# State space recurrence on one core: the multiply by Cx on another engine, loads and sums in another order

## The chip, the cores and the metric

The kernel runs on one core of one Trainium2 chip, as a single launch. The core has five engines that work at the same time and meet through semaphores: TensorE (PE) for matmuls, VectorE (DVE) and ScalarE (ACT) for elementwise work, GpSimd (POOL) for elementwise work and some transfers, and SyncE (SP), which here only issues transfers. The metric is the device time of one execution in microseconds (us). Before the change it was 2233.52 us in the median of three runs, 2227.85 to 2237.58.

## The reference

Two batches of 1024 tokens with 128 features pass through eight residual blocks: latent attention, a spiking feed-forward, a state space block, the spiking feed-forward again, linear attention, experts, a softmax attention and the experts again. The change lies in the state space block:

```
A = -jnp.exp(A_log)
def step(h, inp):
    dt, b_t, c_t, x_t = inp
    A_bar = jnp.exp(dt[:, :, None] * A)
    h = A_bar * h + (dt * x_t)[:, :, None] * b_t[:, None, :]
    y = jnp.einsum('ben,bn->be', h, c_t)
    return (h, y)
_, y = jax.lax.scan(step, h0, xs)
y = y.transpose(1, 0, 2)
y = y + x * W_D
y = y * jax.nn.silu(skip)
y = jnp.einsum('ble,de->bld', y, out_w)
return resid + y
```

For each batch there are 256 channels (e) with 16 states (n) each, so 4096 independent recurrences over 1024 tokens.

## The kernel before

The recurrences of a batch are laid out as 32 tiles of 128 rows (8 channels times 16 states) by 1024 tokens. A tile is numbered t here; in its triple (e, s, r), e is the half of the channels, and r and s pick 8 of the half's 128 (rows 32r + 8s onward). Four tiles in a row (r = 0 to 3) form a group.

`StateSpace.loop` handles a tile like this:

- two transfers by SyncE (L759) bring the step sizes, broadcast over the 16 states, into `s_a` (4 buffers) and the inputs into `s_h` (8 buffers), each 512 KB;
- ScalarE makes the decays in place, exp(a * negA) (L768), one tile ahead of the scan;
- VectorE multiplies the inputs by Bx (L799), runs the recurrence as one scan along the tokens (L800) and multiplies the states by Cx (L801), all in place in `s_h`;
- TensorE sums the 16 states of each channel for a whole group with 16 small matmuls (L775, `s_py<-s_h,s_fold`). They are issued in the tile after the group's last. After them the group's four `s_h` buffers are free;
- after four groups `finish` (L785, L788) adds the direct path and multiplies by the gate, on VectorE.

The loads for tile t+3 are issued in tile t, in the order a, h.

The loop does not run alone. The whole first layer stands under a manual schedule: each engine executes its instructions in the order in which the program issues them. `weave` takes one step of the loop, then on average 2.1 steps of a second stream, and so on:

- Batch 0's loop (`space[0].loop`, L1500) has at its side the attention of batch 1 (`latent.attend`) and `late`, which makes the step sizes of the loop's second half (L713 to L724, with two stores by SyncE, L722 and L724, four times). `among` puts one `late` step after two attention steps until they are used up. A unit of attention is one head group c and one block of keys kb: matmuls L359 and L368, an exponential on ScalarE (L382, in two parts), for a diagonal block two selects on POOL (L385), and two units later the weighing and denominator matmuls on TensorE (L418, L401). The first half of the queries has 16 units, all diagonal; the second has 32, of which 16 are. At the end of a half come a reciprocal (L443), matmuls L450 and multiplies L454 or L458 on VectorE.
- Batch 1's loop (L1510) has at its side `late` and what is left behind batch 0: the end of its linear attention (L914 to L917, with an add on POOL, L917) and the first experts. An expert step is three matmuls of 128x512 (L963, L964, L979), a gate on ScalarE (L966) and a product on VectorE (L971), which reads one operand from PSUM.

What follows batch 1's loop, from about 1003 us on, is bound by TensorE: two more attentions and experts, in an order written out by hand.

Of the kernel before, what the change touches and what calls it, by code (L numbers as in the profile page):

```python
# [9 lines left out]
F32 = mybir.dt.float32  # L10
# [9 lines left out]
P = 128  # L20
B = 2
L = 1024
# [588 lines left out]
class StateSpace:  # L611


    EB, R, S, N, CH = 2, 4, 4, 16, 512
# [128 lines left out]
    def loop(self, work, bank):  # L743

        self.bank = bank
        g, w, nc, b, CH = self.g, self.w, self.g.nc, self.b, self.CH
        EB, R, S, N = self.EB, self.R, self.S, self.N
        chunks = [(n, bass.ts(n, CH)) for n in range(2)]

        yg = self.xc  # L750
        tiles = [(e, s, r) for e in range(EB) for s in range(S) for r in range(R)]

        def load(e, s, r):
            pages = []
            a = work.tile([P, L], F32, name="s_a", bufs=4)
            h = work.tile([P, L], F32, name="s_h", bufs=8)
            for k, t in enumerate((a, h)):
                rows = self.steps[e][k, 32 * r + 8 * s : 32 * r + 8 * s + 8, :]
                nc.sync.dma_start(  # L759
                    out=t, in_=rows.unsqueeze(0).to_broadcast([N, 8, L])  # L760
                )
                pages.append(t)
            return pages

        def decay(t, a):
            e, s, r = tiles[t]
            k = (e * R + r) * S + s
            nc.scalar.activation(a, a, AF.Exp, scale=self.shared.negA[:, k : k + 1])  # L768

        def sums(e, s, hcs):  # L770
            if s == 0:
                self.py = [self.bank("s_py") for _ in range(2)]
            for n, cols in chunks:
                for r in range(R):
                    nc.tensor.matmul(  # L775
                        self.py[n][32 * r : 32 * r + 32, :],
                        self.shared.fold[:, s, :],
                        hcs[r][:, cols],
                        start=(s == 0),
                        stop=(s == S - 1),  # L780
                    )

        def finish(e):
            for n, cols in chunks:
                nc.vector.scalar_tensor_tensor(  # L785
                    yg[:, e, cols], self.xc[:, e, cols], w["W_D"][:, e, :], self.py[n], ALU.mult, ALU.add
                )
            nc.vector.tensor_mul(yg[:, e, :], yg[:, e, :], self.gate[:, e, :])  # L788

        ahead = [load(*tiles[t]) for t in range(3)]  # L790
        decay(0, ahead[0][0])
        done, hcs = None, []
        for t, (e, s, r) in enumerate(tiles):
            if t + 3 < len(tiles):
                ahead.append(load(*tiles[t + 3]))
            a, h = ahead.pop(0)
            if t + 1 < len(tiles):
                decay(t + 1, ahead[0][0])
            nc.vector.tensor_mul(h, h, self.Bx)  # L799
            nc.vector.tensor_tensor_scan(h, a, h, 0.0, ALU.mult, ALU.add)  # L800
            nc.vector.tensor_mul(h, h, self.Cx)  # L801
            hcs.append(h)
            if done is not None:
                sums(*done)
                if done[1] == S - 1:
                    finish(done[0])
                done = None
            if r == R - 1:
                done, hcs = (e, s, hcs), []
            yield  # L810
        sums(*done)
        finish(EB - 1)
        yield
        for n, cols in chunks:
            po = self.bank("s_po").rearrange("p (a b) -> p a b", a=4)
            for t in range(4):
                for e in range(EB):
                    nc.tensor.matmul(
                        po[:, t, :],
                        yg[:, e, bass.ts(4 * n + t, P)],  # L820
                        w["out_wT"][:, e, :],
                        start=(e == 0),
                        stop=(e == EB - 1),
                    )
            xn = g.x[:, b * TPB + 4 * n : b * TPB + 4 * n + 4, :]
            nc.vector.tensor_add(xn, xn, po)
            yield
# [802 lines left out]
```

## Time and profile before

The profiled execution has a span of 2232.4 us, 1.1 us under the median of the runs. TensorE's mean granted clock in it was 0.940.

| engine | busy us | share | instructions |
|---|---|---|---|
| PE | 1966.3 | 88% | 13504 |
| DVE | 1656.4 | 74% | 1955 |
| ACT | 1303.7 | 58% | 1698 |
| POOL | 873.1 | 39% | 432 |

| operation | count | us each | sum us |
|---|---|---|---|
| L799 DVE multiply by Bx | 64 | 1.22 (median) | |
| L800 DVE scan | 64 | 2.323 (mean) | 148.7 |
| L801 DVE multiply by Cx | 64 | 1.225 (median) | |
| L768 ACT decays | 64 | 1.149 (median) | |
| L385 POOL selects in batch 0's loop | 64 | 1.366 (mean) | 85.8 |
| L854 POOL add, 128x1024 | 2 | 2.348 (mean) | 4.7 |
| L678 POOL add, 128x512 | 4 | 1.264 (median) | 5.1 |
| loads of s_a, to landing | 64 | 5.2 (median) | |
| loads of s_h, to landing | 64 | 6.5 (median) | |

How to read it: a busy share is a mean over stages with different limits, so a stage's own stretch must be looked at. In a timeline line the first number is the start in us from the beginning of the span, the second the duration, then engine, source line, operation, output and inputs by tile name, shapes, and a count; what stands in brackets is the idle time of the engine before it and what ended it. In a line of waits the three numbers are us in total, number of waits and the longest. A stretch's line gives the busy us (and instructions) of PE, PE's weight loads, DVE, ACT and POOL, then the granted TensorE clock, the busy share of the DMA engines and GB/s.

### The profile page before, as it was taken

How to read it: one execution, taken by the hardware profiler on the slowest of the kernel's cores; microseconds unless marked ns; L12 is line 12 of the kernel's file. 1: busy time of each engine (PE TensorE's matmuls, PEld its weight loads, DVE VectorE, ACT ScalarE, POOL GpSimd, SP SyncE). 2: the span in 40 equal slices, each digit the busy share in tenths (PEclk: the TensorE clock that was granted, in tenths of full speed). 3: DMA queues.
4: the chain of work that ended last, by engine and by line, in shares of the span. 5: the costliest groups of instructions: out<-in, count | busy, mean ns of one | idle time of the engine just before them, and what ended most of it. 6: DMA issues, size and time to landing. Idle time of an engine off the chain costs nothing. (4 is left out here: it accounts for less than half of the span.)

```text
span 2232.4 us, 33571 instructions
## 1 busy us (share of the span) xinstructions
PE 1966.3 (88%) x13504; PEld 1131.1 (51%) x13504; DVE 1656.4 (74%) x1955; ACT 1303.7 (58%) x1698; POOL 873.1 (39%) x432
## 2 busy tenths in 40 slices
PE   7779888979967758897788999999999999999999
PEld 4323243323334323344555667676676667766754
DVE  5866867898774699885325889888898889988322
ACT  1026612266633666754445888778888788877322
POOL 0013400064311000000100777777888778777500
PEclk9779978989998979998899999999999999999999
DMA  4000000197623287530002555665666656565200
GB/s 90 1 1 1 1 1 0 35 224 166 158 70 104 60 201 172 134 74 0 1 0 66 152 151 152 153 164 147 156 159 157 161 153 158 152 156 151 48 5 5
DMA packets 73787, 219.98 MB, mean 99 GB/s; under 512 B 9184, under 2 KB 19872, under 8 KB 73504
## 3 DMA queue, kind: packets, MB, share of 16 engines
q1 hardware_dynamic: 54736, 149.40, 22.8%
q0 software_dynamic: 18432, 67.12, 15.9%
q8 instruction: 106, 1.74, 0.3%
q10 hardware_dynamic: 464, 1.33, 0.3%
q14 instruction: 49, 0.40, 0.1%
HBM read 78.35 MB, written 5.24 MB: 37 GB/s over the span
## 5 line engine op out<-in xcount | busy, mean ns | idle before, releaser
L1277 POOL TENSOR_TENSOR h_e<-h_e,h_r 128x2048 f32<-128x2048 f32 x128 | 601.8, 4705 | 66.9 <-issue 60.4
L1248 DVE TENSOR_REDUCE h_m<-h_s 128x128 f32<-128x2048 f32 x128 | 292.8, 2288 | 88.8 <-PE h_s L1237 88.8
L1254 DVE TENSOR_TENSOR h_e<-h_s,h_m 128x2048 f32<-128x2048 f32 x128 | 293.2, 2291 | 9.6 <-DVE h_m L1248 0.4
L1269 PE MATMUL h_pd<-h_e,ident 128*128 128x256 f32 x1024 | 250.9, 388 | 25.8 <-DMA h_e<-h_e 25.4
L1257 ACT ACTIVATE h_e<-h_e 128x1024 f32<-128x1024 f32 x256 | 256.5, 1049 | 28.0 <-DVE h_e L1254 27.2
L1067 ACT ACT_TABLE_LOAD x134 | 171.9, 1283 | 104.6 <-PE e_pgu L1060 103.5
L1269 PEld LDWEIGHTS h_pd<-h_e,ident 128*128 128x128 f32 x1024 | 191.3, 192 | 63.6 <-issue 39.6
L385 POOL TENSOR_SCALAR_AFFINE_SELECT a_pT<-a_pT 128x256 f32<-128x256 f32 x120 | 130.3, 1108 | 206.7 <-ACT a_pT L382 203.8
L287 DVE TENSOR_REDUCE a_nm<-a_s 128x2 f32<-128x1024 f32 (+7 forms) x144 | 168.2, 1218 | 45.6 <-PE a_s L278 27.3
L1060 PE MATMUL e_pgu<-e_uT,Wg 128*128 128x256 f32 x640 | 196.4, 389 | 5.4 <-DVE e_h L1075 2.4
L1075 DVE TENSOR_TENSOR e_h<-e_sg,e_pgu 128x256 f32<-128x256 f32 x320 | 119.8, 404 | 106.7 <-ACT e_sg L1067 103.8
L1265 POOL DMA_DIRECT2D h_e<-h_e x128 | 114.4, 894 | 201.5 <-DMA h_e<-h_e 69.6
L1060 PE MATMUL e_pgu<-e_uT,Wu 128*128 128x256 f32 x640 | 192.5, 383 | 0.0
L1085 PE MATMUL h_po<-e_h,Wd 128*128 128x256 f32 x640 | 186.7, 408 | 3.5 <-DVE e_h L1075 2.3
L1067 ACT ACTIVATE e_sg<-e_pgu 128x256 f32<-128x256 f32 x320 | 112.3, 382 | 105.9 <-PE e_pgu L1060 90.4
L382 ACT ACTIVATE a_pT<-a_st 128x1024 f32<-128x1024 f32 (+3 forms) x176 | 129.9, 791 | 67.6 <-PE a_st L368 66.1
L1257 ACT ACT_TABLE_LOAD x128 | 164.2, 1283 | 2.3
L1085 PEld LDWEIGHTS h_po<-e_h,Wd 128*128 128x128 f32 x640 | 111.7, 193 | 102.3 <-issue 76.3
L800 DVE TENSOR_TENSOR_SCAN s_h<-s_a,s_h 128x1024 f32<-128x1024 f32 x64 | 148.7, 2323 | 18.0 <-ACT s_a L768 14.1
L269 PE MATMUL a_s<-a_latT,a_qT 32*128 32x512 f32 (+3 forms) x768 | 123.2, 621 | 39.3 <-DVE a_nm L287 37.4
L1237 PE MATMUL h_s<-h_qz,h_kT 32*128 32x512 f32 x1024 | 147.6, 646 | 9.8 <-DVE h_e L1254 7.9
L1282 PE MATMUL h_po<-h_e,h_vz 128*32 128x128 f32 x4096 | 138.4, 276 | 3.6 <-DVE x_res L1375 3.4
(290 smaller groups left out, 3066.2 us busy)
## 6 DMA issues: line engine op xcount, KB each, us to landing
h_e<-h_e SPq DMA_DIRECT2D x128, 512.0 KB, 4.7
h_e<-h_e POOLq DMA_DIRECT2D x128, 512.0 KB, 4.6
s_a<-s_steps SPq DMA_DIRECT2D x64, 512.0 KB, 5.2
s_h<-s_steps SPq DMA_DIRECT2D x64, 512.0 KB, 6.5
s_steps<-s_gate SPq DMA_DIRECT2D x8, 256.0 KB, 2.0
Wg<-in_Wg_dram SPq DMA_DIRECT2D x8, 256.0 KB, 6.0
Wu<-in_Wu_dram SPq DMA_DIRECT2D x8, 256.0 KB, 5.9
Wd<-in_Wd_dram SPq DMA_DIRECT2D x8, 256.0 KB, 6.1
```

The source lines that it names most:

```text
L287: nc.vector.tensor_reduce(nm[:, half, i, h : h + together], s[:, :, :n], AX.X, ALU.max, negate=True)
L800: nc.vector.tensor_tensor_scan(h, a, h, 0.0, ALU.mult, ALU.add)
L1060: nc.tensor.matmul(pgu[:, k, :], w[name][:, e, f], uT, start=True, stop=True)
L1067: nc.scalar.activation(sg, pgu[:, 0, :], AF.Silu)
L1085: nc.tensor.matmul(self.sums, self.w["Wd"][:, e, fc, :], h, start=False, stop=last, skip_group_check=True)
L1237: nc.tensor.matmul(s[:, j, :].rearrange("p (k q) -> p k q", k=K), kTs[b][quad, bass.ts(kb, P)], qzs[b][qb // 4][quad, :, bass.ts(qb % 4, P ...
L1248: nc.vector.tensor_reduce(m, heads.rearrange("p h q -> p q h"), AX.X, ALU.max)
L1254: nc.vector.tensor_sub(e, heads, m.unsqueeze(1).to_broadcast([P, H, P]))
L1257: nc.scalar.activation(eh, eh, AF.Exp, scale=scale)
L1269: nc.tensor.matmul(pd, g.ident, pair[:, :, k, :], start=(k == 0), stop=(k == 7))
L1277: nc.gpsimd.tensor_mul(e, e, r.unsqueeze(1).to_broadcast([P, H, P]))
L1282: nc.tensor.matmul(po[32 * j : 32 * j + 32, :], vz[:, kb * J + j, k].rearrange("p a d -> p (a d)"), a[:, 4 * j + k, :], start=False, stop= ...
```

## The change

Three things in `StateSpace.loop`:

- the multiply of the states by Cx is issued to POOL instead of VectorE;
- `load` brings one of the two pages; in tile t first the inputs of tile t+2, then the step sizes of tile t+3 are issued;
- a group's sums are issued in the second tile after its last one (r == 1 of the next group) instead of the first; with them `finish` of the first half of the channels. The last group's sums still stand directly after the loop.

```
-        def load(e, s, r):
-            pages = []
-            a = work.tile([P, L], F32, name="s_a", bufs=4)
-            h = work.tile([P, L], F32, name="s_h", bufs=8)
-            for k, t in enumerate((a, h)):
-                rows = self.steps[e][k, 32 * r + 8 * s : 32 * r + 8 * s + 8, :]
-                nc.sync.dma_start(
-                    out=t, in_=rows.unsqueeze(0).to_broadcast([N, 8, L])
-                )
-                pages.append(t)
-            return pages
+        def load(k, e, s, r):
+            t = work.tile([P, L], F32, name="s_h", bufs=8) if k else work.tile([P, L], F32, name="s_a", bufs=4)
+            rows = self.steps[e][k, 32 * r + 8 * s : 32 * r + 8 * s + 8, :]
+            nc.sync.dma_start(out=t, in_=rows.unsqueeze(0).to_broadcast([N, 8, L]))
+            return t
...
-        ahead = [load(*tiles[t]) for t in range(3)]
-        decay(0, ahead[0][0])
+        decays, inputs = [], []
+        for t in range(3):
+            decays.append(load(0, *tiles[t]))
+            if t < 2:
+                inputs.append(load(1, *tiles[t]))
+        decay(0, decays[0])
         done, hcs = None, []
         for t, (e, s, r) in enumerate(tiles):
+            if t + 2 < len(tiles):
+                inputs.append(load(1, *tiles[t + 2]))
             if t + 3 < len(tiles):
-                ahead.append(load(*tiles[t + 3]))
-            a, h = ahead.pop(0)
+                decays.append(load(0, *tiles[t + 3]))
+            a, h = decays.pop(0), inputs.pop(0)
             if t + 1 < len(tiles):
-                decay(t + 1, ahead[0][0])
+                decay(t + 1, decays[0])
             nc.vector.tensor_mul(h, h, self.Bx)
             nc.vector.tensor_tensor_scan(h, a, h, 0.0, ALU.mult, ALU.add)
-            nc.vector.tensor_mul(h, h, self.Cx)
+            nc.gpsimd.tensor_mul(h, h, self.Cx)
             hcs.append(h)
-            if done is not None:
+            if r == 1 and done is not None:
                 sums(*done)
                 if done[1] == S - 1:
                     finish(done[0])
```

## The prediction

> **What bounds the kernel now.** I read the page first, then busy time by stage for the stretches in which the changed loop runs, then VectorE's and POOL's timelines there, then the waits. Batch 0's loop runs from 450 to 662 us (attention of batch 1 beside it), batch 1's from 778 to 1003 us (experts beside it).
>
> ```profile
> span 2232.4 us, 33571 instructions
> ```
> ```profile
> core 0: us, PE busy (x) PEld busy (x) DVE busy (x) ACT busy (x) POOL busy (x), PEclk, DMA share, GB/s
> 450.00:517.00 67.00, 57.32 (x512) 20.04 (x514) 64.59 (x46) 47.44 (x62) 46.81 (x32) 0.87 0.97 226
> 517.00:640.00 123.00, 115.31 (x1022) 42.98 (x1022) 92.45 (x63) 72.90 (x90) 40.87 (x33) 0.99 0.62 146
> 778.00:821.00 43.00, 17.82 (x46) 7.08 (x46) 40.69 (x42) 24.42 (x29) 4.36 (x2) 0.67 0.92 214
> 821.00:1003.00 182.00, 165.07 (x444) 66.02 (x445) 161.49 (x155) 128.76 (x137) 0.00 (x0) 0.96 0.56 132
> ```
> Four regimes: VectorE sets the pace in 450-517 and 778-821 (96% and 95% busy), TensorE in 517-640 (94%); in 821-1003 the two are nearly level. POOL is free in batch 1's loop, but has 64 selects (L385) in batch 0's, half of them in its first 67 us.
>
> A tile with nothing between it and the next, and one with two expert products between:
> ```profile
> 652.76 1.22 DVE L799 TENSOR_TENSOR s_h<-s_h,s_Bx 128x1024 f32<-128x1024 f32 x1
> 654.08 2.29 DVE L800 TENSOR_TENSOR_SCAN s_h<-s_a,s_h 128x1024 f32<-128x1024 f32 x1
> 656.41 1.23 DVE L801 TENSOR_TENSOR s_h<-s_h,s_Cx 128x1024 f32<-128x1024 f32 x1
> 657.55 1.22 DVE L799 TENSOR_TENSOR s_h<-s_h,s_Bx 128x1024 f32<-128x1024 f32 x1
> ```
> ```profile
> 963.35 2.29 DVE L800 TENSOR_TENSOR_SCAN s_h<-s_a,s_h 128x1024 f32<-128x1024 f32 x1
> 965.68 1.22 DVE L801 TENSOR_TENSOR s_h<-s_h,s_Cx 128x1024 f32<-128x1024 f32 x1
> 966.82 1.28 DVE L971 TENSOR_TENSOR e_h<-e_sg,e_pu 128x512 f32<-128x512 f32 x2
> 968.02 1.22 DVE L799 TENSOR_TENSOR s_h<-s_h,s_Bx 128x1024 f32<-128x1024 f32 x1
> ```
> The Cx multiply takes 1.15 us from start to next start; the whole bare tile 4.79.
>
> **Price of the multiply on POOL.** The trace has POOL tensor-tensor rows of the same shape, and two places where a smaller one meets the loop:
> ```profile
> L854 POOL TENSOR_TENSOR l_u<-l_u,b_out 128x1024 f32<-128x1024 f32 x2 | 4.7, 2348 | 297.0 <-ACT l_un L84 297.0
> ```
> ```profile
> 784.49 1.22 DVE L799 TENSOR_TENSOR s_h<-s_h,s_Bx 128x1024 f32<-128x1024 f32 x1
> 784.65 2.18 POOL L917 TENSOR_TENSOR x_res<-x_res,l_u 128x512 f32<-128x512 f32 x1 [25.09 <-DVE l_u L916]
> ...
> 785.81 3.17 DVE L800 TENSOR_TENSOR_SCAN s_h<-s_a,s_h 128x1024 f32<-128x1024 f32 x1
> ```
> ```profile
> 545.46 1.88 POOL L471 TENSOR_TENSOR x_res<-x_res,a_rs 128x512 f32<-128x512 f32 x1 [1.33 <-ACT a_rs L470]
> ...
> 546.31 2.11 DVE L801 TENSOR_TENSOR s_h<-s_h,s_Cx 128x1024 f32<-128x1024 f32 x1
> ```
> POOL's 512-element add takes 1.26 alone (L678) but 2.18 here: it waits out L799, and then the scan takes 3.17 instead of 2.29. The second place repeats it with 2.11 for 1.23. So the two engines take turns on operations with two SBUF inputs, and a POOL add of 1.26 costs VectorE 0.88, its length less 0.38. The multiply of 2.35 then costs 1.97. Products that read one side from PSUM do not collide: L1277 on POOL keeps 4.7 for twice the size while VectorE runs L1254 undisturbed at 2.29.
>
> The Trainium skill ("SBUF — State Buffer", the section Summary: rules for kernel authors) goes further: the second operation blocks until the first has finished entirely. The rows show 0.38 less. By the rule each bare tile would lose another 0.38, an estimated 5 us over the sum; I keep the rows.
>
> **Sum by tile type.** Bare tile: VectorE loses 1.15 and waits 1.97, **+0.8**. Two expert products (1.2) between: POOL starts at the end of the scan and holds the next L799 until 2.3 (0.08 to start, 2.35 less 0.14 overlap) after it, where L799 started 2.4 after it: **-0.1**. More than 2.3 of harmless work or waiting between: **-1.15**. With batch-0 late sizes between: L717 reads one SBUF input and hides, L718/L719 must wait for POOL, 2.3+1.4 against 3.3, +0.4; L721 goes ahead of POOL and L723 behind, 0.7+2.1+0.7 against 2.75, +0.75.
>
> *450-517.* Tiles 0 to 10: seven bare (5.6), two each of the late kinds (0.8+1.5): VectorE is 7.9 late. TensorE feels it, because POOL works in order: the selects of attention units issued after tile t now wait behind multiply t, which waits for scan t; the weighing matmuls L418 wait for the selects, and everything after them on TensorE. The last selects of this half ended at 515.4. Now: scan 10 ends at 510.1+7.1, the next L799 goes first (1.2), multiply 2.35, two selects with one scan between (0.4+2.3+0.4) give 523.9, **+8.5**. If the six selects queued before it each wait out one VectorE operation at the contended mean of 1.37 us, it is about +12. I take **+10**; bounds +2 (TensorE keeps its lead) and +20 (43 POOL operations against some 30 of VectorE, which alternate).
>
> *517-640.* TensorE-bound; one head group takes 25.6 us (L434 at 577.33 and 602.91). The shared turn would hold 3.8 tiles x (3.51+1.97) + 8 selects x 0.41 = 24.2 of these. Selects that ended at 575.4 come some 4 later by laying operations in turn, in the next group 2.5; with quieter groups counted at less, +2 for each of four groups: **+8**; bounds 0 and +16. L458, on TensorE's way at 632, stands behind one multiply fewer: **-1**. The tail to 663 mixes -1.15 and +0.8: 0.
>
> *778-821.* Types sum to -0.3: **0**.
>
> *821-1003.*
> ```profile
> PE e_pu L964 <- DVE e_h L971: 19.8, 13, 7.0
> ```
> This row caps the gain: nothing VectorE gives back can exceed TensorE's 19.8 of waiting for it. Ten ordinary tiles at -0.1, one with statistics -1.15, one with the finish -0.3 make -2.5. Ten tiles where VectorE itself waits for ScalarE or TensorE could give -10 but TensorE paces them; I credit 1.5. **-4**, bounds -20 and +2.
>
> *Fetches and sums.* SyncE's order stays a, h, a, h; a pair leaves when scan t-4 is done (a at 453.55, h at 454.11 after the scan ending 453.52). Only the h next to a store (L722/L724) falls behind it, with three tiles (15 us) against 6.5 us to land: 0. If that cover went, a late h would cost up to its 6.5 at each of the eight places. The sums one tile later free eight h buffers a tile later, still three tiles before use; they meet multiply t+3's POOL latency (2.35 against 1.23), so TensorE's 4.2 us of waiting there in 450-517 is replaced by the selects' wait, counted above. After 1003 TensorE's order and work are unchanged and the difference is carried through.
>
> Total 10+8-1-4 = **+13**: the profiled execution, 2232.4 of span, becomes 2245.4. The median of the runs, 2233.5, is 1.1 over that span, so **2246 us**.
>
> **Rivals.**
> 1. *TensorE's lead absorbs the turns* (2234, chance 0.36). For it: TensorE waits only 4.2 for this loop in 450-517, and VectorE idles 30 of 123 us in 517-640. Against: order on POOL. Half 0 +5, groups +0, loop 2 -4, tail -1: +0.
> 2. *Faster: POOL's turns fall under expert products and VectorE hands them over sooner* (2218, chance 0.10). Place: 821-1003. For it: 55 products of 0.68 there do not collide and POOL is empty. It needs nearly all of the 19.8: -18, with batch 0 at +2. It decides if TensorE's waits on L971 fall below 5 us. Against: between scans 2.3 replaces 2.4.
> 3. *Selects starve* (2266, chance 0.12). POOL gets one operation per VectorE operation: +20 and +16, with -1 and -3. For it: 1.37 mean against 0.41 uncontended. Against: VectorE stalls when ScalarE's decays are late, and lets POOL through.
>
> **Numbers.** Forecast chance 0.42. About 0.5% (11 us) is what a measurement here can tell from no change. Slower by more: 0.42+0.12 = 0.54; within: 0.36; faster: 0.10. The range reaches down into rival 1 by the measured spread (2228) and up nearly to rival 3's time (2264).
>
> **What would show it.** L801 on POOL near 2.4 alone and above 3.5 where it waits; L800 or L799 long by 2; selects above 1.4; batch 0's loop ending near 680, batch 1's loop 4 shorter. Wrong if L800 stays at 2.29 with POOL busy, or if L418 does not wait on POOL.

## The result, and the profile after

The changed kernel takes 2250.46 us in the median of 12 runs (2231.71 to 2259.72), the kernel before 2230.11 in the median of 12 runs beside them (2224.41 to 2245.99). The medians are 20 us apart; the ratio between the two kernels' runs is 1.0072, with a 95% interval of 1.0048 to 1.0095: slower, by 16 us in 2230 (11 to 21). The profiled execution of the changed kernel has a span of 2249.1 us, against 2232.4 before. The page of the profile after, its head (busy us, share of the span, instructions) and the groups of the scan, of the multiply that moved and of the selects (out<-in, count | busy us, mean ns of one | idle before and what ended it):

```profile
span 2249.1 us, 33636 instructions
...
PE 1960.4 (87%) x13504; PEld 1128.8 (50%) x13504; DVE 1636.0 (73%) x1891; ACT 1303.9 (58%) x1698; POOL 1024.6 (46%) x496
...
L801 POOL TENSOR_TENSOR s_h<-s_h,s_Cx 128x1024 f32<-128x1024 f32 x64 | 171.1, 2675 | 266.5 <-DVE s_h L800 245.2
...
L800 DVE TENSOR_TENSOR_SCAN s_h<-s_a,s_h 128x1024 f32<-128x1024 f32 x64 | 168.7, 2637 | 25.7 <-ACT s_a L762 21.9
...
L385 POOL TENSOR_SCALAR_AFFINE_SELECT a_pT<-a_pT 128x256 f32<-128x256 f32 x120 | 111.9, 954 | 74.8 <-ACT a_pT L382 72.1
```

VectorE gave up 64 multiplies, 79.6 us in sum, but its busy time fell by only 20.4 (1656.4 to 1636.0). By the groups of both profiles the scans grew by 20.0 (148.7 to 168.7), the multiplies by Bx by 25.5 (80.7 to 106.2) and the late sizes L718 to L723 by 11.7: 57 of the missing 59 us are VectorE instructions of the same work that took longer, which is what waiting for turns with POOL looks like. POOL took on 171.1 us for work that fills 64 x 2.35 = 150.

The loops are cut here at the same events in every kernel: the first multiply by Bx, the reciprocals L443 that end the two halves of the attention, the end of the second L826 (the loop's result added in; a changed kernel's line may be a few lower) and, for batch 1, from its first multiply by Bx to its first L826. "Half 0" and "half 1" are the stretches that the prediction called 450-517 and 517-640, "tail" is the rest of batch 0's loop, "loop 2" batch 1's. The cuts are made at the starts in the timelines, the second L826 at its end; "repeat" is a later run of the changed kernel (an experiment below).

| us | half 0 | half 1 | tail | loop 2 | sum of changes |
|---|---|---|---|---|---|
| before | 67.9 | 106.9 | 50.6 | 227.0 | |
| after | 84.7 | 110.5 | 46.5 | 223.7 | |
| change | +16.8 | +3.7 | -4.1 | -3.3 | +13.1 |
| repeat | 83.3 | 109.6 | 52.0 | 223.6 | |
| change | +15.4 | +2.7 | +1.4 | -3.4 | +16.1 |

The loss lies in half 0. (The rounding of the cuts is 0.1.) Outside the loops the profile after differs too: 8.0 less before the loop and 14.9 more in the last softmax attention, both in code that the change does not touch. The repeat has 4.0 less and 3.2 more there, and over all the profiles of this case the attention takes 868 to 889 us, so these look like differences between executions.

The stretches half 0, half 1, tail and loop 2 of the profile after (us; busy us and instructions of PE, PEld, DVE, ACT, POOL; granted clock, DMA share, GB/s), and then half 0 and half 1 of the one before:

```profile
441.93:526.58 84.65, 66.14 (x514) 23.21 (x516) 65.19 (x35) 48.08 (x63) 69.79 (x44) 0.74 0.82 192
526.58:637.08 110.50, 105.32 (x968) 37.04 (x964) 75.49 (x38) 68.93 (x86) 78.50 (x48) 0.97 0.56 131
637.08:683.60 46.52, 28.95 (x148) 16.21 (x148) 38.23 (x42) 13.56 (x17) 13.43 (x6) 0.89 0.35 89
785.90:1009.60 223.70, 181.81 (x505) 74.91 (x506) 189.54 (x164) 152.98 (x166) 81.03 (x34) 0.89 0.62 149
```
```profile
449.90:517.80 67.90, 58.12 (x516) 20.26 (x516) 64.72 (x48) 48.18 (x63) 46.81 (x32) 0.87 0.98 227
517.80:624.70 106.90, 104.40 (x968) 37.11 (x964) 81.25 (x54) 68.90 (x86) 40.87 (x33) 1.00 0.65 152
```

In half 0 VectorE's busy time is the same although 13 instructions are gone (48 to 35), and POOL's has gone from 46.8 to 69.8 us. No engine is busy for nine tenths of the stretch any more.

VectorE's timeline at the start of half 0 (start, us, engine, line, operation), then POOL's:

```profile
443.25 2.29 DVE L800 TENSOR_TENSOR_SCAN s_h<-s_a,s_h 128x1024 f32<-128x1024 f32 x1
445.46 1.20 DVE L799 TENSOR_TENSOR s_h<-s_h,s_Bx 128x1024 f32<-128x1024 f32 x1
446.76 4.25 DVE L800 TENSOR_TENSOR_SCAN s_h<-s_a,s_h 128x1024 f32<-128x1024 f32 x1
```
```profile
445.62 3.24 POOL L801 TENSOR_TENSOR s_h<-s_h,s_Cx 128x1024 f32<-128x1024 f32 x1 [65.46 <-DVE s_h L800]
448.81 6.63 POOL L385 TENSOR_SCALAR_AFFINE_SELECT a_pT<-a_pT 128x256 f32<-128x256 f32 x4
455.41 2.79 POOL L801 TENSOR_TENSOR s_h<-s_h,s_Cx 128x1024 f32<-128x1024 f32 x1
```

The multiply waits out the next L799 (3.24 instead of 2.35), then the next scan waits for the multiply (4.25 instead of 2.29), and the four selects behind it in POOL's queue wait in turn for VectorE's operations: 6.63 us for four, where one alone takes 0.41.

The waits of half 0 (us, number, longest), 441 to 527 us after:

```profile
PEld a_oT L418 <- POOL a_pT L385: 21.5, 13, 5.9
PE a_oT L418 <- POOL a_pT L385: 13.4, 5, 5.5
DVE a_rec L443 <- ACT a_rec L442: 11.2, 1, 11.2
DVE s_xc L719 <- ACT s_xc L716: 7.1, 2, 3.8
```

Before, TensorE waited 0.2 us for the selects in this half, and its weight loads 2.8. Now the weighing matmuls stop for up to 5.5 us at a time, VectorE is idle 11.2 us before the reciprocal that closes the half, and for 7.1 us in the late sizes. The two idle times of VectorE do not show a loss by themselves: the kernel further down in which POOL only writes has 8.2 and 7.1 us at the same places and its half 0 is as short as before.

### The profile page after: what moved, and what is told of

The parts are those of the page before. It is cut to its first block, busy times and chain, and to the rows that moved or that the text cites. A ratio compares the mean times of both kernels' runs of the same rounds, so it can differ in the third digit from the quotient of the medians.

```text
span 2249.1 us, 33636 instructions
## 1 busy us (share of the span) xinstructions
PE 1960.4 (87%) x13504; PEld 1128.8 (50%) x13504; DVE 1636.0 (73%) x1891; ACT 1303.9 (58%) x1698; POOL 1024.6 (46%) x496
## 5 line engine op out<-in xcount | busy, mean ns | idle before, releaser
L801 POOL TENSOR_TENSOR s_h<-s_h,s_Cx 128x1024 f32<-128x1024 f32 x64 | 171.1, 2675 | 266.5 <-DVE s_h L800 245.2
L800 DVE TENSOR_TENSOR_SCAN s_h<-s_a,s_h 128x1024 f32<-128x1024 f32 x64 | 168.7, 2637 | 25.7 <-ACT s_a L762 21.9
L269 PE MATMUL a_s<-a_latT,a_qT 32*128 32x512 f32 (+3 forms) x768 | 116.1, 579 | 43.3 <-DVE a_nm L287 41.4
L385 POOL TENSOR_SCALAR_AFFINE_SELECT a_pT<-a_pT 128x256 f32<-128x256 f32 x120 | 111.9, 954 | 74.8 <-ACT a_pT L382 72.1
```

Source lines behind the costliest of these rows:

```text
L801: nc.gpsimd.tensor_mul(h, h, self.Cx)
```

## The experiments

Each ratio is to the kernel before, run beside it, with its 95% interval. In all but the first and the last but one, the fetches and the sums stand as in the change. Cx stands for the multiply L801.

### Which part costs

**Cx alone** (loads and sums as before):
```
-            nc.vector.tensor_mul(h, h, self.Cx)
+            nc.gpsimd.tensor_mul(h, h, self.Cx)
```


> The multiply by Cx goes to POOL and nothing else changes; loads and sums stay as before the change. Theory (turns on SBUF inputs, and the selects' place behind the multiplies on POOL): batch 0's loop from its first Bx multiply to the first reciprocal (67.9 us before the change, 84.7 with it) stays at 82 to 92, since TensorE now also stands at the sums until POOL's multiply of 2.35 us is done; the time is 1.005 to 1.012 of before. Rival (the later fetch or the later sums cost it): that stretch falls back to under 73 and the time to within 0.3% of before.

Ratio 1.0091 (1.0059 to 1.0123), half 0 83.3, half 1 113.5. **Loads and sums alone**, with Cx on VectorE:
```
-            nc.gpsimd.tensor_mul(h, h, self.Cx)
+            nc.vector.tensor_mul(h, h, self.Cx)
```


> Loads and sums as in the change, the multiply by Cx on VectorE as before it. Theory: neither costs or gains more than 2 us: the stretch to the first reciprocal 66 to 70 us, batch 1's loop from its first Bx multiply to its first residual addition 225 to 229 (227.0 before), the time within 0.2% of before. Rival (fetching the inputs only two tiles ahead starves the loop): the scan or the Bx multiply waits for loads and the two loops are 5 to 15 us longer together.

Ratio 0.9996 (0.9973 to 1.002). The whole loss comes with the multiply; the new order by itself shows no cost within the 0.3% of its interval. In the stretches it does shift time: half 1 is 104.2 with it (106.9 before) and the tail 56.6 (50.6). The later sums take a wait away, whichever engine multiplies: TensorE waits ahead of the small matmuls for 19.4 us in the kernel before (6 waits, for VectorE's multiply), for 19.1 (5 waits, for POOL's) with Cx alone and for 2.4 (1 wait) in the change; half 1 is 113.5 with Cx alone and 109.6 to 110.5 in the change.

**Cx on POOL in one batch only**, batch 1 and then batch 0:
```
-            nc.gpsimd.tensor_mul(h, h, self.Cx)
+            (nc.gpsimd if b else nc.vector).tensor_mul(h, h, self.Cx)
```


> The whole change, but in batch 0's loop the multiply by Cx stays on VectorE. Theory: batch 0's loop as before the change (67.9, 106.9 and 50.6 us for its three stretches, each within 2), batch 1's loop 223 to 225 against 227.0: the time 0.998 to 1.000 of before, 3 to 4 us less. Rival 1 (the loss is general contention, also in batch 1): 1.003 or more. Rival 2 (the 15 us that the profile after the change shows in the unchanged softmax attention belongs to the change): the attention's stretch (870.8 before, 885.6 after) is long here too.

> The whole change, but in batch 1's loop the multiply by Cx stays on VectorE. Theory: the loss stands whole in batch 0's loop, 82 to 87 us to the first reciprocal, 108 to 113 between the reciprocals, 45 to 48 after; batch 1's loop 226 to 228; the time 1.006 to 1.011 of before, 3 us above the change's own. Rival (the loss lies in batch 1's loop or after it): within 0.3% of before.

In batch 1 alone: 0.999 (0.9963 to 1.0017), loop 2 223.8. In batch 0 alone (`nc.vector if b else nc.gpsimd`): 1.009 (1.0055 to 1.0125), half 0 83.3, half 1 109.7, loop 2 227.3. So the loss is batch 0's. Batch 1's loop is some 3 us shorter with the multiply on POOL; in the time of the whole kernel that gain is within the interval.

**The change again**, one execution:

> The change once more, for a second profile. Theory: the stretches of batch 0's loop (84.7, 110.5, 46.5) and of batch 1's (223.7) come back within 3 us; the softmax attention's (885.7) does not have to, since its transfers set it, and lies anywhere from 868 to 886. Rival: the attention is long again, above 880, and the change lengthens it.

Span 2245.7 and the last attention 874.0 us (885.7 in the profile after, 870.8 before). The same kernel gives 885.7 and 874.0, and the run with POOL in batch 1 alone has 871.4: nothing here shows that the change lengthens the attention, though one more execution does not rule out a few us.

### What in half 0

**Writes in the multiply's place.** In batch 0 the multiply by Cx is left out, and as much POOL time put there that reads nothing:
```
-            nc.gpsimd.tensor_mul(h, h, self.Cx)
+            if b:
+                nc.gpsimd.tensor_mul(h, h, self.Cx)
+            else:
+                for _ in range(2):
+                    nc.gpsimd.memset(h, 0.0)
+                nc.gpsimd.memset(h[:, 0:CH], 0.0)
```


> The change, but in batch 0's loop POOL writes zeros over the states (two and a half memsets, some 2.2 us by the memset rows of the trace) instead of multiplying them by Cx; batch 0's multiply by Cx is thereby left out. POOL's order and the wait for each scan stay, but the POOL operation reads nothing from SBUF. Theory (turns are taken over reads of SBUF): scans stay at 2.3 us with no 4.25 among them, VectorE goes through its tiles 2 us faster, and the stretch to the first reciprocal falls from 84 to 67 to 74. Rival 1 (any POOL operation of that length holds VectorE): scans of 4 us stay, the stretch too. Rival 2 (the selects' place behind the scan is what costs, whatever the length of VectorE's tile): scans at 2.3, but the stretch stays above 79.

Ratio 0.9984 (0.9965 to 1.0004), half 0 67.6. VectorE's and POOL's timelines in this kernel:

```profile
446.57 2.29 DVE L800 TENSOR_TENSOR_SCAN s_h<-s_a,s_h 128x1024 f32<-128x1024 f32 x1
```
```profile
445.42 1.96 POOL L805 MEMSET s_h<- 128x1024 f32 x2 [65.44 <-DVE s_h L800]
447.43 0.52 POOL L806 MEMSET s_h<- 128x512 f32 x1
447.92 3.21 POOL L385 TENSOR_SCALAR_AFFINE_SELECT a_pT<-a_pT 128x256 f32<-128x256 f32 x4
```

The scan keeps 2.29 while POOL writes, and the three memsets take 0.95 + 0.95 + 0.52 = 2.43 us, about the multiply's 2.35. The place in POOL's queue, the wait for the scan and the POOL time are those of the change, and nothing is lost; what is gone is the taking of turns, and the selects run 27.9 us in sum. The Trainium skill ("SBUF — State Buffer", the section Who interferes with whom) says that a VectorE instruction with two SBUF inputs collides with a GpSimd instruction that reads SBUF and not with one that only writes; the two scans, 4.25 and 2.29, agree.

**The multiply one tile later**, so that POOL finds the scan done and does not hold the selects while it waits:
```
-            nc.gpsimd.tensor_mul(h, h, self.Cx)
+            if b:
+                nc.gpsimd.tensor_mul(h, h, self.Cx)
+            elif t > 0:
+                nc.gpsimd.tensor_mul(last, last, self.Cx)
+            last = h
```
(with the last one after the loop)

> The change, but in batch 0's loop the multiply of tile t is issued to POOL in tile t+1, so that the selects of tile t's attention units no longer wait for scan t, only for scan t-1. Theory (half of the loss is the turns, half the order): turns stay, scans of 4.25 us are still there, TensorE's 13.4 us of waiting for selects to the first reciprocal falls below 7, and that stretch is 74 to 80 instead of 84.7 (83.3 in another run of the same loop). Rival 1 (order alone): below 71. Rival 2 (turns alone): 82 or more.

Ratio 1.005 (1.0029 to 1.007), half 0 79.4: 4 to 5 us of half 0 hang on POOL's wait for the scan, some 12 stay. TensorE's wait for the selects is down from 13.4 us to 4.2, so most of the loss is not in that row; POOL's gaps are down from 6.7 us to 0.3. The later multiply brings a wait of its own, 5.6 us of TensorE ahead of the small matmuls.

**No multiply on POOL ahead of the late sizes.** VectorE's idle 7.1 us at L719 suggested a ring that I had not counted: L719 waits for ScalarE's logarithm L716, queued behind exponentials that wait for TensorE, which waits for selects, which wait for POOL's multiply, which waits for VectorE.
```
-            nc.gpsimd.tensor_mul(h, h, self.Cx)
+            (nc.vector if t in (2, 7) and not b else nc.gpsimd).tensor_mul(h, h, self.Cx)
```


> The change, but in batch 0 tiles 2 and 7, the ones after which the late sizes' logarithm L716 and sums L717 to L719 follow, keep Cx on VectorE. Theory (the missing term of half 0 is the ring: VectorE's L719 waits for ScalarE's L716, that for exponentials, these for TensorE, that for selects, these for POOL's multiply of the same tile): VectorE's waits on L716 fall from 7.1 to under 2, half 0 from 83.3 to 74 to 78, ratio about 1.004 to 1.006. Rival (the turns slow all tiles evenly, the waits on L716 only show it): two of eleven tiles fewer take 2 x 1.5 off, half 0 80 to 82, ratio about 1.007.

Ratio 1.0046 (1.0024 to 1.0069), and the theory of the ring falls. VectorE's wait for L716 is down to 1.3 us, but half 0 is still 82.0 (and the kernel with writes had that wait, 7.1 us, without the loss). Its waits and POOL's groups in half 0, 440 to 527 us (for the groups from 447):

```profile
DVE s_xc L719 <- ACT s_xc L716: 1.3, 1, 1.3
...
PEld a_oT L418 <- POOL a_pT L385: 26.8, 18, 4.6
...
PE a_oT L418 <- POOL a_pT L385: 16.6, 11, 4.2
```
```profile
L385 POOL TENSOR_SCALAR_AFFINE_SELECT a_pT<-a_pT 128x256 f32<-128x256 f32 x32 | 42.4, 1356 | 1.9 <-ACT a_pT L382 1.9
L801 POOL TENSOR_TENSOR s_h<-s_h,s_Cx 128x1024 f32<-128x1024 f32 x10 | 30.1, 3005 | 68.8 <-DVE s_h L800 68.8
```

The 68.8 us are POOL's idle time ahead of the first multiply. From there to the end of the last one in this half its stretch reads

```profile
451.34:525.05 73.71, 56.06 (x466) 19.71 (x468) 64.44 (x34) 41.56 (x57) 71.80 (x42) 0.81 0.90 207
```

POOL is busy for 71.8 of 73.7 us, and all of its idle time there is the 1.9. Two multiplies fewer take 5.0 us off its work, and the selects grow by 7.0 (32 of them: 35.4 us after, 42.4 here), probably since VectorE, which no longer stops for L716, has more operations to take turns with. **From the first multiply on, POOL's own queue, its turns included, fills the stretch.** That is read from POOL's busy share in this run; in the change itself POOL is busy for 82 to 86% of half 0, and no run parts POOL's waiting for turns from VectorE's. Side by side:

| half 0 | us | POOL busy us | POOL operations | PEclk |
|---|---|---|---|---|
| before | 67.9 | 46.8 | 32 selects | 0.87 |
| writes in its place | 67.6 | 56.0 | 32 selects, 36 memsets | 0.80 |
| multiply later | 79.4 | 75.3 | 32 selects, 12 multiplies | 0.81 |
| not at tiles 2 and 7 | 82.0 | 71.8 | 32 selects, 10 multiplies | 0.81 |
| repeat of the change | 83.3 | 71.8 | 32 selects, 12 multiplies | 0.81 |
| after | 84.7 | 69.8 | 32 selects, 12 multiplies | 0.74 |

Without contention the changed half's POOL work would be 12 x 2.35 + 32 x 0.41 = 41 us. The rest up to 70 is waiting for turns; with the multiply issued later POOL fills its half best (75.3 of 79.4), since it no longer stands idle for scans.

### What the rest is worth

**Cx on POOL from half 1 on** (batch 0 from tile 11, all of batch 1):
```
-            nc.gpsimd.tensor_mul(h, h, self.Cx)
+            (nc.gpsimd if b or t > 10 else nc.vector).tensor_mul(h, h, self.Cx)
```


> The change, but batch 0's first 11 tiles (first half of the queries) keep Cx on VectorE; batch 0's tiles 11 to 31 and all of batch 1 have it on POOL. It prices the prediction's step 517-640 (+8) by itself. Base: the run with loads and sums alone had half 0 67.0, half 1 104.2, tail 56.6. Theory (that step was over-sized; VectorE's stalls let POOL through): half 0 67, half 1 108 to 110, tail 51 to 53, so batch 0's loop within 2 us of that base, batch 1's loop 3 to 4 shorter than 227; ratio to before 0.997 to 1.002. Rival (the small +3 was seen only because half 0 was already late): half 1 112 or more, ratio 1.002 to 1.006.

Ratio 0.9974 (0.9951 to 0.9998), half 0 65.6, half 1 110.1, tail 46.5. Half 1 takes some 3 us more than before and the tail 4 us less: together 156.6, against 157.5 before and 160.8 with loads and sums alone. Two executions of the changed kernel differ by more there (157.0 and 161.6), so half 1 and tail together are level, not shown to gain. Neither theory had the tail at 46.5; all four profiles with a tail of 46.5 had a granted clock of 0.89 in it, and the 56.6 of loads and sums alone stood at 0.73. Most of the 6 us gained is in loop 2: 221.9, 5.1 less than before (expected 3 to 4).

**Cx on POOL in batch 1 from tile 9 on**, past the stretch 778-821 where VectorE sets the pace, first with the loads and sums of the change and then with those of before:
```
-            nc.gpsimd.tensor_mul(h, h, self.Cx)
+            (nc.gpsimd if b and t > 8 else nc.vector).tensor_mul(h, h, self.Cx)
```


> The change with POOL taking the multiply by Cx only in batch 1's loop and only from its tile 9 on, where two expert products lie between the tiles. Theory: the bare tiles at its start lose nothing any more, batch 1's loop is 220 to 224 (223.8 with POOL in all its tiles, 227.0 before), batch 0's as before the change; the time 0.996 to 1.000 of before. Rival (the gain comes from the early tiles): 225 to 228.

> The kernel before, with only Cx on POOL in batch 1 from tile 9 on; loads and sums in the old order. Theory (loads and sums are worth nothing but POOL's latency makes TensorE wait for the sums in their old place): loop 2 222 to 225 against 220.2 with both, tail back to about 50.6; ratio 0.997 to 1.000. Rival (the sums' place does not matter in batch 1): loop 2 about 220, tail 50.6, ratio 0.994 to 0.997, and the loads and sums should be left as they were.

(In the second kernel the line stood on VectorE.) With the new order 0.9976 (0.9956 to 0.9996), loop 2 220.2; with the old one 0.9991 (0.9968 to 1.0015), loop 2 221.8. The two intervals overlap: whether the order is worth anything here stays open, in loop 2 it would be 1.6 us.

**Both together**:
```
-            nc.gpsimd.tensor_mul(h, h, self.Cx)
+            (nc.gpsimd if t > (8 if b else 10) else nc.vector).tensor_mul(h, h, self.Cx)
```


> The change, with Cx on POOL only where neither the selects of the first half (batch 0, tiles 0 to 10) nor VectorE's own pace (batch 1, tiles 0 to 8) stand against it. Theory (POOL's own queue paces only the first half, everywhere else the change gains or is level): half 0 about 66, half 1 plus tail 155 to 157 (157.5 before), loop 2 220 to 221 (227.0 before); ratio to before 0.994 to 0.9975, at or under the best so far (0.9974 and 0.9976). Rival (the gains do not add, TensorE takes the earlier finish of batch 0's loop back in the stretch between the loops): ratio 0.998 to 1.0.

2225.59 us against 2235.51 beside it: ratio 0.9953 (0.9933 to 0.9973), faster than both kernels and the lowest ratio here, though its interval overlaps those of its two parts (0.9974 and 0.9976). Half 0 65.7, half 1 and tail 156.4, loop 2 218.7 (expected 220 to 221); TensorE's waits for the expert products in all of loop 2, 775.8 to 994.5 us:

```profile
PE e_pu L964 <- DVE e_h L971: 13.8, 9, 6.0
```

That row was 19.8 before, 14.8 to 18.0 in the kernels with all of batch 1's multiplies on POOL, and 13.3 in the two above with POOL from tile 9 on. The gain that the prediction's second rival looked for in loop 2 is there in part (8.3 us). Leaving out the early tiles is only some of it, because loop 2 also goes with the granted clock. All kernels side by side, with the clock of the tail, and that of loop 2 from its 43rd us on:

| us | half 0 | half 1 | tail (clock) | loop 2 (clock) | the four, against before | ratio, in us |
|---|---|---|---|---|---|---|
| before | 67.9 | 106.9 | 50.6 (0.87) | 227.0 (0.96) | | |
| after | 84.7 | 110.5 | 46.5 (0.89) | 223.7 (0.95) | +13 | +16 |
| repeat | 83.3 | 109.6 | 52.0 (0.77) | 223.6 (0.96) | +16 | |
| Cx alone | 83.3 | 113.5 | 49.2 (0.79) | 225.4 (0.95) | +19 | +20 |
| loads and sums alone | 67.0 | 104.2 | 56.6 (0.73) | 228.0 (0.96) | +3 | -1 |
| POOL in batch 1 only | 67.0 | 104.2 | 56.6 (0.73) | 223.8 (0.95) | -1 | -2 |
| POOL in batch 0 only | 83.3 | 109.7 | 52.0 (0.77) | 227.3 (0.96) | +20 | +20 |
| writes in its place | 67.6 | 105.9 | 53.3 (0.74) | 221.5 (0.97) | -4 | -4 |
| multiply later | 79.4 | 109.7 | 51.7 (0.77) | 223.8 (0.95) | +12 | +11 |
| not at tiles 2 and 7 | 82.0 | 110.6 | 46.5 (0.89) | 220.3 (0.98) | +7 | +10 |
| POOL from half 1 on | 65.6 | 110.1 | 46.5 (0.89) | 221.9 (0.97) | -8 | -6 |
| batch 1 from tile 9 | 66.9 | 104.2 | 53.4 (0.78) | 220.2 (0.96) | -8 | -5 |
| the same, old order | 66.9 | 106.9 | 50.6 (0.87) | 221.8 (0.95) | -6 | -2 |
| both together | 65.7 | 109.9 | 46.5 (0.89) | 218.7 (0.98) | -12 | -11 |

The four stretches account for the measured ratios to within 5 us, which is about what the ratios' own intervals leave. With every multiply of batch 1 on POOL, loop 2 lies between 220.3 and 223.8; from tile 9 on, in the new order, it is 3.4 shorter at a clock of 0.96 (220.2 against 223.6) and 1.6 at 0.98 (218.7 against 220.3).

## Why the prediction was right, and where its steps were not

The forecast was slower by 13 us, 2246; by the ratio it is slower by 16, and the median is 2250. The sign, the place and the mechanism (turns between the two engines, selects late behind the multiply) held. That the sum of the terms came so near is in part luck: in the profile after, half 0 cost 6.8 us more than its term, half 1 and the tail 4.3 and 3.1 less, and the four stretches again make +13. Step by step:

- **The price of a turn, 1.97 on VectorE.** Measured 1.96: 4.25 for the scan less 2.29. The prediction took the rule that the second operation blocks until the first has finished as 0.38 us more than the rows show; that reading was wrong. The scan was issued at 446.76; the multiply, if its last 2.35 us are its work, had begun at 446.51. The scan ended at 451.01, and a scan of 2.29 us that started at the multiply's end (448.86) would have ended at 451.15. The rows differ from the rule by 0.14 us, and those from L917 likewise by 0.14 (788.98 against 789.12). The rest of the 0.38, some 0.25 us, is how much later the second operation came than the first. A repeated pair of small collisions in the trace of before was enough to price a large one.
- **Two expert products between, -0.1.** VectorE's timeline of the changed kernel, and the multiply on POOL:
```profile
957.81 2.29 DVE L800 TENSOR_TENSOR_SCAN s_h<-s_a,s_h 128x1024 f32<-128x1024 f32 x1
960.01 1.34 DVE L971 TENSOR_TENSOR e_h<-e_sg,e_pu 128x512 f32<-128x512 f32 x2
961.27 2.44 DVE L799 TENSOR_TENSOR s_h<-s_h,s_Bx 128x1024 f32<-128x1024 f32 x1
963.75 2.29 DVE L800 TENSOR_TENSOR_SCAN s_h<-s_a,s_h 128x1024 f32<-128x1024 f32 x1
```
```profile
960.27 2.36 POOL L801 TENSOR_TENSOR s_h<-s_h,s_Cx 128x1024 f32<-128x1024 f32 x1 [3.58 <-DVE s_h L800]
```
  From scan to scan 5.94, and L799 is stretched to 2.44 by the multiply that began with the products. Before, a tile of this kind took 5.92: no gain, about as worked out. **Loop 2, -4:** -3.3 (-3.4 in the repeat), though other kernels with the same loop 2 lie 5 to 7 us under the one before. TensorE's wait for L971 went from 19.8 to 16.0 (17.9 in the repeat), so rival 2 does not hold.
- **Half 0, +10: the mis-sized term.** It measured +16.8 (+15.4 in the repeat). I summed how late VectorE would be (7.9) and let the last few selects queue behind it. VectorE's lateness came out near that, its last scan of the half ending 8.2 us later, but most of it is idle time at L719 that the sum did not have. The last selects of the half and the reciprocal that ends it, before and then after:
```profile
507.95 7.41 POOL L385 TENSOR_SCALAR_AFFINE_SELECT a_pT<-a_pT 128x256 f32<-128x256 f32 x4
517.77 3.35 DVE L443 RECIPROCAL a_rec<-a_rec 128x512 f32<-128x512 f32 x1 [1.33 <-ACT a_rec L442]
```
```profile
519.00 0.77 POOL L385 TENSOR_SCALAR_AFFINE_SELECT a_pT<-a_pT 128x256 f32<-128x256 f32 x2
526.58 3.35 DVE L443 RECIPROCAL a_rec<-a_rec 128x512 f32<-128x512 f32 x1 [11.16 <-ACT a_rec L442]
```
  Counted from the start of the half, the last select ended at 65.4 us before and at 77.8 after, +12.4; from there to the reciprocal it was 2.4 us and is 6.8, +4.4 (+3.3 in the repeat). The first part is POOL: 32 selects and 12 multiplies that wait for turns make 70 us of queue, which starts with the first multiply, 3.7 us into the half, with 6.7 us of gaps (three waits of 2.2 for a scan) in the profile after and 1.9 in the run without the two tiles. The closing estimate of that step, about +12 with 1.37 a select, was this part. The second part, TensorE's and ScalarE's work after the last select, the prediction let move along unchanged; what lengthens it was not tried. The upper bound of +20 (43 POOL operations taking turns) was nearer than the term, and I took it for a bound, because VectorE's tile sum came to less. The ring over L716 adds little, as the run without it showed.
- **Half 1, +8: too large.** +3.7 (+2.7 in the repeat), given back in the tail of the profile after but not in the repeat's. Part of the smallness is the new order: against the kernel with loads and sums alone (104.2) the multiply costs 5.4 to 6.3 in half 1, and the tail then takes 5 to 10 less than that kernel's. My laying of operations in turn took VectorE as always active; it waits for ScalarE's decays there (21.9 us against 14.1 before, L800 on the decays), and POOL gets through: TensorE waits 3.1 us for the selects in half 1, where half 0 has 13.4. Rival 3, starving selects, came nearer in half 0 and was wrong for half 1.
- **The tail, 0, and L458, -1.** At a like clock (0.87 before, 0.89 after) it took 4.1 less, so this was under-sized there; in the repeat, at 0.77, it is 1.4 longer than before.
- **Fetches and sums, 0:** 0.9996 alone, with half 1 shorter and the tail longer in its profile.
- **Of the signs named beforehand,** L801 near 2.4 alone and a scan longer by 2 came, and L418 waits on POOL; batch 0's loop ended at 683.6 and batch 1's was 3.3 shorter. L801 where it waits takes 3.24 at first and up to 4.35, not always above 3.5. "Selects above 1.4" did not: in half 0 they average 1.14, less than the 1.49 before, perhaps as VectorE itself is held more often. A shorter select was no sign that POOL had time.
- **L717, counted as hiding,** was held (see the end).

What stays open: why the granted clock of half 0 is 0.74 in the profile after and 0.81 in the repeat of the same kernel, and that of the tail 0.89 and 0.77. TensorE's busy time goes with it (66.1 and 61.9 us for the same 514 matmuls in half 0), and so does the length of the tail and of loop 2 in the table above; what sets it was not tried. The run with writes in the multiply's place has 0.80 and still the short half, so a clock of 0.8 alone does not lengthen it.

## What to carry to other kernels

When work is moved to an engine that executes in order, price that engine's own queue in the stretch where it is already used: its operations times their contended durations, beside the lateness of the engine relieved, and then what still follows its last operation. Where two engines take turns, a moved operation is worth something only in the tiles in which other, harmless work or waiting covers the turn; here it cost 15 to 17 us in one half of one loop, and kept out of that half (and out of nine tiles of the other loop) the same line, with the new order of loads and sums, gained 0.5%. An idle wait that the trace shows may be the echo of a bound elsewhere: take it away by itself before it goes into the sum.

## What the runs showed of the hardware

- A POOL operation that only writes left VectorE alone: the scan kept 2.29 us beside memsets (0.95 us for 128x1024 in f32), and took 4.25 beside the multiply.
- An f32 tensor-scalar with one SBUF input was held as well. L717, which I had counted as hiding, takes 0.62 us in the kernel with loads and sums alone; with the multiply one tile later, VectorE's timeline has, beside a multiply on POOL from 454.17 to 458.49,
```profile
456.26 2.51 DVE L717 TENSOR_SCALAR s_gate<-s_xc 128x512 f32<-128x512 f32 x1
```
- The granted clock moved between executions in stretches where TensorE waits much: 0.74 and 0.81 in half 0, 0.77 and 0.89 in the tail, for one and the same kernel, and the tail differed by 5.5 us.
